# A perceiver block on one core: the way up's first rooms, its opening transposes, and who computes its weights' low parts

## The chip, the cores and the metric

The kernel runs on one core of one Trainium2 chip. Its time is the device time of one execution in microseconds (us), and the median of several executions is what counts. The core has a matmul engine (TensorE, PE in the profile, with PEld its weight loads), three engines for elementwise work (VectorE or DVE, ScalarE or ACT, GpSimd or POOL), a queue engine (SyncE or SP) that issues most transfers, and 16 DMA engines that move data between the large memory and the core's own memory. Each engine works through its own list of instructions in order and waits on semaphores for the others.

## The reference

The block takes `x` (32 sequences of 64 rows of 512 numbers, 2048 rows in all) and adds three things to it in turn.

```python
x = x + xattn(layernorm(x), ctx_2048, mask)        # cross attention
x = x + attn(layernorm(x), wq_a, ..., wo)          # latent attention, 16 heads
x = x + ffn(layernorm(x), gate_w, up_w, down_w, expert_weight, gamma, beta)

def ffn(h):
    logits = h @ gate_w                            # 8 experts
    scale = top_k(logits, 2).sum()
    hidden = square(relu(h @ up_w))                # 512 -> 2048: the way up
    shared = hidden @ down_w                       # 2048 -> 512: the way down
    y = shared + (h @ expert_weight) * scale       # the expert
    return (y - mean(y)) * rsqrt(var(y) + 1e-5) * gamma + beta
```

All of it is float32. The change lies in the last line's `ffn`.

## The kernel before, in words

**Precision.** A float32 number is kept as a high and a low part in a format that PE multiplies quickly. `split` makes them: ACT copies the number into the high part (rounding it), and another engine subtracts that from the number for the low part. A product of two such numbers takes three matmuls: high by high, low by high, high by low. `mm3` writes these three for the expert.

**Fewer products.** Large matrix products are computed in the manner of Strassen and Winograd, with seven products of blocks where eight would be needed. That costs sums ahead of them (`sums`, on POOL, or on `xc` for the way up in `sum_x`) and sums behind them (`combine`: one ACT copy and five DVE additions, lines 160 to 168, in four steps).

**Stages.** Cross attention and the latent attention's heads come first. Then come three products with a weight matrix each: the output projection (`wo`, tiles `op` and `oo`), the way up (`up`, tiles `up` and `uo`) and the way down (`down`, tiles `dp` and `do`). Each matrix lies in eight weight slots, each with seven blocks of high parts (`wh_...`) and seven of low parts (`wl_...`). `read_slot` brings a slot's seven blocks from the large memory into the room of its low parts, and `put_slot` then splits them in two pieces, of blocks 0 to 3 (1024 numbers in each of 128 rows) and 4 to 6 (768). The order in which a stage uses the slots is `ORDER = (0, 1, 5, 6, 7, 2, 3, 4)`. A slot is filled for the next stage while the stage before still runs on others.

**The way up.** It runs through four blocks of 512 rows (`b`), and in each through the eight slots (`n`, with slot `k = ORDER[n]`). One such unit (`up_seven`) is 42 matmuls of 256 columns, which are written to one of two sets of four accumulator banks. In unit 0 of a block, four of the seven sums first get five of their six products, so that the last part of `xr` is needed late. Behind each unit come `combine`, then relu and square on ACT (lines 1226 and 1227, tile `uo`), then for most slots the sums for the way down on POOL (`uw`), and the stores of `uo` and `uw`. `xr` are the high and low parts of the rows, made by `right(b, part)`: parts 0 and 1 are high and low of one half, 2 and 3 of the other; high parts are ACT's, low parts DVE's. Inside the first block, slots 3 to 7 in `ORDER` are split behind units 0 to 4. Inside the last block, the way down's first five slots are split behind units 2 to 6.

**The way down.** Its unit `u` is 21 matmuls, on a pair `hl` (high and low parts of a piece of `uo`, split by `left(u)`) and a slot of `down`. `left(0)`, `left(1)` and `left(2)` are written inside the way up's last block, behind units 3, 5 and 6; `left(u + 3)` is written at the way down's unit `u`.

**Settling.** `settle(n, ...)` writes `n` transposes into an accumulator bank that nobody reads. It stands ahead of the way up's first unit with eight of them, and ahead of units 5 and 32 of the way down with four.

**Order.** The kernel is written in a framework that orders the instructions of each engine by their place in the source and by a model of when they can start; so an instruction that is ready early may move ahead of others. `with after(ins)` or a `pins` argument holds an instruction behind another one of the same engine: the first pin is for ACT's copy, the second for the subtraction. The framework sets all semaphores. It also gives every tile its room: a pool's tags take their places in the order in which they are first used, and the rooms of a pool that is closed go to later pools. A write into such a room waits until the last reader of the tile before, a transfer among them, is done.

**The rooms of the way up.** The projection's pool `o_act` holds, in this order, `beb`, `mo`, `xt`, `o`, `p1`, `xn` (also `oT`), `xh`, `xl`. The tile `mo` is the expert's output and is written out from ACT's queue (line 1023); it is taken for the first time ahead of all others (`mos`, line 1070). When `o_act` is closed, the pool `f_act` takes the first of its rooms: three for `uo` of 5 KB a row and two for `up1`. The first `uo` then lies over `beb` and the start of `mo`; the later `u_x` rooms lie over `xh`, `xl` and what follows.

**The seam.** The last rows of the projection are turned (`o_t`, tiles `ops`, `oh`, `ol`, `oT`), the expert runs on them (`o_expert`, tiles `cpe`, `gs`, `mo`), and the way up begins with unit 0 of block 0. Its `right(0, 3)` waits for the expert's last product, since it writes over the expert's weights.

## Time and profile before

| what | us |
|---|---|
| median of three executions | 1104.6 |
| the three executions | 1100.06, 1104.6, 1104.91 |
| the profiled execution, its own time | 1098.9 |
| its span in the profile | 1096.7 |
| expert's last product begins | 772.9 |
| way up, first product to last | 773.1 to 931.0 |
| way up, last block: units begin at | 891.6, then every 4.95 |
| way down, first unit begins | 931.2 |
| granted PE clock, mean | 0.998 |

The three costliest groups that belong to the seam's stages, from the page's list (line, engine, operation, output and inputs, shapes, count, then busy time and the mean of one in ns):

```profile
L1156 PE MATMUL up<-xr,wh_up 128*128 128x256 f32 x896 | 157.6, 280 | 0.6 <-DVE uo L168 0.6
L1156 PE MATMUL up<-xr,wl_up 128*128 128x256 f32 x448 | 123.7, 280 | 0.0
L725 PE MATMUL dp<-wh_down,hl 128*128 128x256 f32 x448 | 124.5, 278 | 0.0
```

Matmuls overlap one another in the pipeline, so a mean of 280 ns is not the distance of one from the next. Behind the last bar of such a line stands the time for which the engine stood idle just before these instructions, and who ended it. In a timeline, a line has the start, the duration, the engine, the line of the source, the operation, the tiles, and in brackets the idle time before it. In a table of windows the columns are the window, its length, then the busy time and number of instructions of each engine, the granted clock, the DMA engines' share and GB/s.

### The profile page before, as it was taken

The page shows a single profiled execution, that of the slowest core. Times are in us where ns is not written, and L with a number is a line of the kernel's source. Part 1 is how long each engine was busy: PE and PEld are TensorE (multiplying, and loading weights), DVE is VectorE, ACT ScalarE, POOL GpSimd, SP SyncE. Part 2 cuts the span into 40 slices and gives each one's busy share as a digit, 9 for nine tenths or more (in the row PEclk, how much of TensorE's full clock was granted, in tenths as well). Part 3 has the DMA queues.
Part 4 walks back from the last instruction along what each step waited for, and adds up shares of the span by engine and source line. Part 5 has one row for each costly group of instructions (what it writes and reads, how often), then busy time and mean ns, then how long its engine had stood idle before and what let it go on. Part 6 is the DMA issues. An engine that isn't in the chain of part 4 may idle for free.

```text
span 1096.7 us, 26072 instructions
## 1 busy us (share of the span) xinstructions
PE 1066.9 (97%) x10201; PEld 983.6 (90%) x10201; DVE 769.0 (70%) x1369; ACT 546.1 (50%) x1051; POOL 508.1 (46%) x691
## 2 busy tenths in 40 slices
PE   8999999999999999999998999999999999999996
PEld 6667777679999999999988999999999999999996
DVE  5666666657666666656787866667785658898786
ACT  4444444533433444434475544445676567755553
POOL 2333333326788778874570000003238970065671
PEclk9999999999999999999999999999999999999999
DMA  8867666343776778655487776779646689998672
GB/s 259 263 216 231 206 212 203 124 161 121 260 234 245 260 247 294 249 207 195 160 324 276 263 241 213 231 235 359 218 156 202 221 247 366 310 309 257 206 232 79
DMA packets 195386, 254.67 MB, mean 232 GB/s; under 512 B 18544, under 2 KB 140032, under 8 KB 195264
## 3 DMA queue, kind: packets, MB, share of 16 engines
q1 hardware_dynamic: 190704, 240.92, 67.0%
q10 hardware_dynamic: 3456, 8.39, 2.2%
q0 software_dynamic: 1104, 3.70, 0.9%
q8 instruction: 80, 1.31, 0.5%
q14 instruction: 42, 0.34, 0.1%
HBM read 146.67 MB, written 106.30 MB: 231 GB/s over the span
## 4 chain that ended last, share of the span: by engine, by line
PE 59%; DMA 10%; POOL 9%; DVE 8%; issue 7%; ACT 5%; SPq 1%; DVEq 0%; POOLq 0%; ACTq 0%
PE up L1156 9%; PE pss L773 5%; PE psq L179 4%; PE psq L180 4%; PE psq L181 4%; PE op L725 3%; PE op L726 3%; PE op L723 3%; PE psv L817 3%; DMA hd<-uo 2%; PE pse L179 2%; PE pse L181 2%; PE pse L180 2%; DMA x1d<-xt 2%; DMA vd<-vw 2%
## 5 line engine op out<-in xcount | busy, mean ns | idle before, releaser
L755 DVE SCALAR_TENSOR_TENSOR qe<-pse,bqp,cq 64x256 f32<-64x256 f32 x256 | 123.7, 483 | 76.5 <-PE pse L181 70.7
L1156 PE MATMUL up<-xr,wh_up 128*128 128x256 f32 x896 | 157.6, 280 | 0.6 <-DVE uo L168 0.6
L1156 PEld LDWEIGHTS up<-xr,wh_up 128*128 128x128 f32 x896 | 137.5, 189 | 1.0 <-issue 0.7
L725 PE MATMUL op<-wh_wo,hl 128*128 128x256 f32 x448 | 124.4, 279 | 3.7 <-DVE hl L149 3.7
L723 PE MATMUL op<-wh_wo,hl 128*128 128x256 f32 x448 | 124.0, 280 | 0.6 <-ACT hl L147 0.6
L725 PE MATMUL dp<-wh_down,hl 128*128 128x256 f32 x448 | 124.5, 278 | 0.0
L723 PE MATMUL dp<-wh_down,hl 128*128 128x256 f32 x448 | 124.4, 278 | 0.0
L726 PE MATMUL dp<-wl_down,hl 128*128 128x256 f32 x448 | 124.3, 277 | 0.0
L149 DVE TENSOR_TENSOR hl<-c,hl 128x896 fp32r<-128x896 f32 x84 | 94.3, 1126 | 42.3 <-ACT hl L147 42.0
L1156 PE MATMUL up<-xr,wl_up 128*128 128x256 f32 x448 | 123.7, 280 | 0.0
L726 PE MATMUL op<-wl_wo,hl 128*128 128x256 f32 x448 | 123.5, 277 | 0.0
L147 ACT CAST hl<-c 128x896 fp32r<-128x896 f32 x84 | 79.0, 942 | 77.7 <-PE op L726 38.0
L179 PE MATMUL psq<-qa_hi,qh 128*128 128x256 f32 x384 | 112.5, 293 | 0.0
L180 PE MATMUL psq<-qa_hi,ql 128*128 128x256 f32 x384 | 106.4, 277 | 0.0
L181 PE MATMUL psq<-qa_lo,qh 128*128 128x256 f32 x384 | 106.2, 276 | 0.0
L725 PEld LDWEIGHTS op<-wh_wo,hl 128*128 128x128 f32 x448 | 84.3, 188 | 4.8 <-DVE hl L149 4.7
L723 PEld LDWEIGHTS op<-wh_wo,hl 128*128 128x128 f32 x448 | 83.6, 188 | 1.5 <-ACT hl L147 0.8
L723 PEld LDWEIGHTS dp<-wh_down,hl 128*128 128x128 f32 x448 | 84.6, 189 | 0.0
L725 PEld LDWEIGHTS dp<-wh_down,hl 128*128 128x128 f32 x448 | 84.1, 188 | 0.4 <-DVE hl L149 0.4
L1156 PEld LDWEIGHTS up<-xr,wl_up 128*128 128x128 f32 x448 | 84.2, 188 | 0.0
L726 PEld LDWEIGHTS op<-wl_wo,hl 128*128 128x128 f32 x448 | 84.1, 188 | 0.0
L726 PEld LDWEIGHTS dp<-wl_down,hl 128*128 128x128 f32 x448 | 84.1, 188 | 0.0
(233 smaller groups left out, 3146.6 us busy)
## 6 DMA issues: line engine op xcount, KB each, us to landing
c<-vd SPq DMA_DIRECT2D x58, 448.0 KB, 4.2
cx<-in_ctx SPq DMA_DIRECT2D x32, 512.0 KB, 4.6
vd<-vw SPq DMA_DIRECT2D x29, 512.0 KB, 3.6
hd<-uo SPq DMA_DIRECT2D x107, 128.0 KB, 3.3
hd<-uw SPq DMA_DIRECT2D x21, 512.0 KB, 3.3
dcw<-hd SPq DMA_DIRECT2D x18, 448.0 KB, 5.6
vd<-v SPq DMA_DIRECT2D x30, 256.0 KB, 3.5
wd_wo<-pw_wo SPq DMA_DIRECT2D x8, 896.0 KB, 4.9
```

Of the source, the lines that this page charges most:

```text
L147: copy = nc.scalar.copy(hi, src)
L149: return copy, engine.tensor_tensor(lo, src, hi.bitcast(FP), ALU.subtract)
L179: nc.tensor.matmul(ps, ah, bh, start=(j == 0), stop=False)
L180: nc.tensor.matmul(ps, al, bh, start=False, stop=False)
L181: nc.tensor.matmul(ps, ah, bl, start=False, stop=(j == n - 1))
L723: first = nc.tensor.matmul(ps[s // 2][:, s % 2], h[:, a], wh[:, b], start=(k == 0 and s % 2 == 0), stop=False)
L725: nc.tensor.matmul(ps[s // 2][:, s % 2], l[:, a], wh[:, b], start=False, stop=False)
L726: ins = nc.tensor.matmul(ps[s // 2][:, s % 2], h[:, a], wl[:, b], start=False, stop=last)
L755: rope = nc.vector.scalar_tensor_tensor(qe[64 * a : 64 * a + 64, :], pe[r, :], bqp[r, p : p + 1], cq[r, a, :], ALU.add, ALU.mult,)
L773: nc.tensor.matmul(ps[64 * j : 64 * j + 64, pj, b, :], qs[2 * pj + j][a][:, sl], kT[:, a, kt], start=(a == 0), stop=(a == 1),)
L817: nc.tensor.matmul(o, kv[a, i, :], t[a, bp, :], start=True, stop=True)
L1156: nc.tensor.matmul(ps[s // 2][:, s % 2], w[:, i, kk], xr[b, 2 * kk + low][:, j], start=(first and m == 0), stop=(last and m == len(parts) ...
```

## The change

Five edits, all around the way up.

1. `mo` isn't taken ahead of the others any more; its tag takes the place behind `xl`, and the tags between move down by its 4 KB a row.
2. `mm3` returns its last matmul; `o_expert` collects them, and the way up's opening transposes, now four, are held behind the last of them.
3. Slot `ORDER[2]` is split behind `right(0, 3)` instead of ahead of the last expert, and slot `ORDER[3]` right after it instead of behind unit 0, with its low part on POOL.
4. Slots `ORDER[5]` and `ORDER[7]` have their low parts on POOL too; they, `ORDER[4]` and `ORDER[6]` are split behind units 1 to 4 as before.
5. In the last block, the way down's slot `ORDER[4]` is no longer split behind unit 6 but at the way down's unit 1, and `left(2)` at its unit 0, held behind the last unit's square.

```diff
@@ mm3 @@
-            nc.tensor.matmul(ps, ah, bl, start=False, stop=(j == n - 1))
+            ins = nc.tensor.matmul(ps, ah, bl, start=False, stop=(j == n - 1))
+        return ins
@@ put_slot @@
-            def put_slot(k, what, pins=(None, None)):
+            def put_slot(k, what, pins=(None, None), engine=nc.vector):
...
-                    split(h[:, a], l[:, a], c[:, a], pins=pins)
+                    split(h[:, a], l[:, a], c[:, a], engine, pins)
@@ o_expert @@
-        mo = mos.pop(blk, None) or ap.tile([P, 2, D], FP, tag="mo", name=f"mo{blk}")
+        mo = ap.tile([P, 2, D], FP, tag="mo", name=f"mo{blk}")
...
-                mm3(pe[:, 0 : c.stop - c.start], [
+                made.append(mm3(pe[:, 0 : c.stop - c.start], [
...
-                ])
+                ]))
@@ the projection @@
-    mos = {0: ap.tile([P, 2, D], FP, tag="mo", name="mo0")}
...
-    put_slot(ORDER[2], "up", pins=xT[2])
     for _ in o_expert(NB - 1, *xT):
         pass
+    ends = made[-1]
@@ up_seven @@
-                with after(settle(8, ps, wh[:, 0, 0], ident2, None) if b == 0 else None):
+                with after(settle(4, ps, wh[:, 0, 0], ident2, ends) if b == 0 else None):
@@ the way up @@
-        right(0, 3)
+        put_slot(ORDER[2], "up", pins=(xT[2][0], right(0, 3)))
+        put_slot(ORDER[3], "up", (xT[2][0], None), nc.gpsimd)
...
-                if b == 0 and n < 5:
-                    put_slot(ORDER[n + 3], "up", pins=pins)
-                if b == NB // 2 - 1 and 1 < n < 7:
+                if b == 0 and 0 < n < 5:
+                    put_slot(ORDER[n + 3], "up", *((pins,) if n % 2 else ((act, None), nc.gpsimd)))
+                if b == NB // 2 - 1 and 1 < n < 6:
                     put_slot(ORDER[n - 2], "down", pins=pins)
...
-                if b == NB // 2 - 1 and n == 6:
-                    left(2, pins=(done[0], done[-1]))
@@ the way down @@
+            if u == 0:
+                left(2, pins=pins)
...
-            if u in (4, 6, 8):
-                put_slot(ORDER[3 + u // 2], "down")
+            if u in (1, 4, 6, 8):
+                put_slot(ORDER[max(4, 3 + u // 2)], "down")
```

More of the change, by code (lines that the diff above doesn't have):

```diff
@@ L1024, in o_expert @@
         yield
-    xr, xc, xw = {}, {}, []
+    xr, xc, xw, made = {}, {}, [], []
     def read_x(b, kk, room=None, behind=None):
```

## The prediction

> **What bounds the kernel.** I began with the page: TensorE (PE) is busy nearly throughout, so nothing can be won but its idle stretches and its pace.

> ```profile
> span 1096.7 us, 26072 instructions
> PE 1066.9 (97%) x10201; PEld 983.6 (90%) x10201; DVE 769.0 (70%) x1369; ACT 546.1 (50%) x1051; POOL 508.1 (46%) x691
> ```

> Of the 29.8 us in which PE is idle, the view of waits puts only one in the stage that the change touches: `PE up L1156 <- DVE uo L168: 0.6`. So I looked at the pace: way up's products in windows of 10 us, and then PE's timeline inside two of them.

> ```profile
> 786.00:796.00 10.00, 10.00 (x87) 10.00 (x86) 1.00 0.46 129
> 826.00:836.00 10.00, 10.00 (x91) 10.00 (x90) 1.00 0.60 203
> 856.00:866.00 10.00, 10.00 (x87) 10.00 (x86) 1.00 0.97 320
> ```

> ```profile
> 790.00 0.40 PE L1156 MATMUL up<-xr,wh_up 128*128 128x256 f32 x2
> ...
> 791.06 0.40 PE L1156 MATMUL up<-xr,wh_up 128*128 128x256 f32 x2
> ...
> 819.73 0.39 PE L1156 MATMUL up<-xr,wh_up 128*128 128x256 f32 x2
> ...
> 821.09 0.39 PE L1156 MATMUL up<-xr,wh_up 128*128 128x256 f32 x2
> ```

> PE is fully busy at a granted clock of 1.00 in all of them, yet 9 products take 1.06 us (117.8 ns each) in the first and 12 take 1.36 us (113.3 ns) in the second. There are two paces. Way up runs at the slow one from 773 to 809, at the quick one to 847, and slow again until 943. PE's timeline shows what moves it:

> ```profile
> 767.01 0.60 PE L713 MATMUL up<-ident,wh_up 128*128 128x128 f32 x4
> 773.04 0.27 PE L713 MATMUL up<-ident,wh_up 128*128 128x128 f32 x1
> 808.87 0.48 PE L1156 MATMUL up<-xr,wh_up 128*128 128x256 f32 x2 [0.57 <-DVE uo L168]
> 943.53 0.60 PE L713 MATMUL dp<-ident,wh_down 128*128 128x128 f32 x4
> ```

> At 943.5 four transposes in a row turn the slow pace to the quick one. Ahead of way up stands only one of the eight (773.04); seven ran earlier, between the expert's products. The stop at 808.87 also left the quick pace; one at 847 left the slow one.

> Then VectorE (DVE) at way up's start, in its timeline:

> ```profile
> 773.34 0.95 DVE L1065 TENSOR_TENSOR xr<-xp,xr 128x768 fp32r<-128x768 f32 x1
> 774.21 1.22 DVE L1065 TENSOR_TENSOR xr<-xc,xr 128x1024 fp32r<-128x1024 f32 x1
> 780.10 0.69 DVE L162 TENSOR_TENSOR uo<-up,up 128x512 f32<-128x512 f32 x1 [4.67 <-ACT up L160]
> ```

> The wait is put down to a copy that ended at 776.9. The last `mod<-mo` store is issued at 774.17 and takes 5.8 us: 780.0. `uo` and `mo` lie over one another in memory, so DVE waits for that store, and the delay runs through units 0 to 7 to the stop at 808.87.

> **Rooms, and the transposes.** With `mo` elsewhere, DVE can begin unit 0's sums when its products allow, at about 777.3; the new neighbour (`oT`'s stores, issued at 768.6 and 769.0, 5.6 us at most) is written out by 774.6, before unit 0's first copy at 776.5. The `mo` store now lies under a later `xr`, not written before 805. Gain for DVE: 2.8 us of waiting. PE gets only its stop: unit 7 took 813.39 - 807.78 = 5.61 us where its neighbours took 4.95, so 0.7 us.

> Transposes: four after the expert's last product, spaced 0.11 us, where one stood: 3 x 0.11 = +0.3 us. The seven that go had filled gaps (PE waited there for `oh` and `ol` anyway), so they give nothing back. If way up then starts at the quick pace, its first eight units take 8 x 42 x 0.1133 = 38.1 us, where the trace has 813.39 - 773.07 = 40.3. The stop is inside that 40.3, so pace and stop together give -2.2, and with the transposes **-1.9**. Bounds: 39.6 + 0.3 us, that is -0.4, if the slow pace stays; -1.9 if not. I take -1.9, because the four at 943.5 are the same instruction in the same number.

> [...]

> **Three low parts on GpSimd (POOL).** Each is one subtraction of 1024 and one of 768 elements. DVE does them in 1.22 + 0.95 = 2.2 us; three leave it. POOL has no such form here. Its nearest rows are 256 elements at 0.74 and 512 at 1.27, so 0.53 per further 256: 2.3 + 1.8 = 4.1 us a slot. That is alone. Against a working DVE, 256 elements cost it 1.25:

> ```profile
> 749.30 2.50 POOL L155 TENSOR_TENSOR xc<-xp 128x256 f32<-128x256 f32 x2 [10.44 <-DMA xp<-xTd]
> 775.21 1.52 POOL L155 TENSOR_TENSOR xc<-xp 128x256 f32<-128x256 f32 x2 [11.11 <-DMA x2d<-oo]
> ```

> Seven such are 8.8 us, the upper bound. I take 5.5, nearer to alone, since DVE is to have gaps. Against the need, with units of 4.76 us from 773.4: slot 3 (weights landed at 762.4, high part from 770.3 on ScalarE (ACT)) is low by 777, needed at 787.7; slot 5 has its high part after unit 2's squares, at about 790.4, and is low by 791.3 + 5.5 = 796.8, needed at 797.2; slot 7 is low by 806.3, needed at 807.3. All hidden, with 0.4 us to spare at slot 5; at 8.8 us slot 5 is 2.9 late and slot 7's second piece about 1. Behind them on POOL wait the sums `xc`, which waited for a landing until 775.2 and now run at 777 to 783 (needed after 800), and unit 5's `uw`, which in the trace began only at 808. POOL is idle from 781.7 to 808: that is the cover.

> Moving slot 2's low part behind `right(0,3)` on DVE: done at 777.5 instead of 773.4, needed at 782.9: nothing. But `right(0,3)` (ends 775.4, first needed there) now meets POOL. DVE's 1.22 became 1.75 beside POOL at 812.4, its 0.95 became 1.13: up to 0.7 us late. The first piece is needed first, so I take 0 and keep 0.7.

> [...]

> **Fewer splits at the end.** In the trace unit 2 of the way down starts at 936.1 and finds its `hl` long ready:

> ```profile
> 928.50 0.95 ACT L147 CAST hl<-hl 128x896 fp32r<-128x896 f32 x1
> ...
> 932.80 1.14 ACT L1227 ACTIVATE uo<-uo 128x512 f32<-128x512 f32 x2
> 933.84 1.77 ACT L147 CAST wh_down<-wl_down 128x1024 fp32r<-128x1024 f32 x2
> ```

> Now this split is pinned behind the last unit's squares. DVE, free of one `hl` part (1.0), does that unit's sums at 932.0 to 934.35. ACT squares from 934.0 to 936.2, then the high part to 937.1, the low part on DVE to 938.15. Unit 2's second product needs it at 936.2: **+2.0 us** of standing, where before nothing stood. Bounds: 0 if the squares come 2 us earlier; 3.0 if another 0.95 us split is put ahead. Behind it on ACT the splits for units 3 and 4 end at 938.8 and the moved weights' high part (1.77) at 940.6, the low part (2.1) by 942.7; unit 4 then starts at about 943: no further wait. The reads keep their places in the queues.

> **Sum**: -1.9 + 0 + 2.0 = **+0.1 us**, about no change. On the profiled execution (1098.9 us around its span of 1096.7) that is 1099. But this one was the fastest: 1098.9, 1100.06, 1104.6 and 1104.91 have a mean of 1102.1, under the median of 1104.6. I put the forecast there: **1102 us**, its own range 1098 to 1106.

> Forecast, 0.50: as summed.

> Rival 1, 0.22, faster: the quick pace holds. Units 16 to 31 take 79.1 us in the trace; at 38.6 a block of eight (the second block's time, its small stop at 847 included) they take 77.3, and without stops 76.2: -1.8 to -3.0. The way down's first five units give 12.27 - 11.9 = -0.4. If the split at its end also costs nothing, the whole is -4.1 to -5.3, 1097 to 1098. Against it: the stop at 847 came out of the second block's own order (DVE stood 3.8 us for POOL's `uw`), which the change leaves as it is.

> Rival 2, 0.14, slower: GpSimd's parts come late. Deciding point: slot 5 low after 797.2, that is over 5.9 us a slot. At 8.8: 2.9 + 1 + 0.7 for `right(0,3)`, with 3.0 at the way down: -1.9 + 7.6 = +5.7, 1108. For it: 2.50 for two beside a busy DVE; against: the 26 us gap of POOL, and DVE's relief.

> Rival 3, 0.14: the transposes don't set the pace. Then -0.4 + 2.0 = +1.6, 1104.

> **Range** 1096 to 1109: from rival 1 with a lucky pace to rival 2. About 0.5% (5.5 us) is what a measurement of this kernel can tell from no change; from 1104.6 that is 1099.1 and 1110.1. Below: most of rival 1 and a tail of the forecast, 0.27. Above: the upper part of rival 2 against the median and other stops, 0.15. Between: 0.58.

> **What would show it.** PE's timeline with four transposes between the expert's last and way up's first product, then 91 products in 10 us; DVE's first sums near 777.5; POOL's subtractions near 2.5 and 2 us; a wait of PE for `hl` some 5 us into the way down. I am wrong if the first eight units still take 40 us, if PE waits for a `wl_up` of POOL, or if no wait stands at the way down's unit 2.

## The result, and the profile after

The changed kernel takes 1111.55 us in the median, the kernel before 1103.55 beside it: a ratio of 1.0078, 95% interval 1.0061 to 1.0095. So it is slower by some 8 us, where I had forecast no change. The profiled execution took 1109.51 us, its span against that of before:

```profile
span 1107.7 us, 26068 instructions
```

I cut both spans at the same instructions of PE's timeline (the start of a unit is the start of its first product; "last turn" is the start of the last transpose of `ops`, after which only the expert's products come):

| stretch | before, us | after, us | difference |
|---|---|---|---|
| start to last turn | 765.64 | 764.38 | -1.3 |
| last turn to way up's first product (the seam) | 7.44 | 9.27 | +1.8 |
| way up, first block, units 0 to 6 | 34.71 | 33.79 | -0.9 |
| first block, unit 7 | 5.60 | 8.14 | +2.5 |
| second block | 38.63 | 39.65 | +1.0 |
| third block, fourth block | 79.15 | 79.51 | +0.4 |
| way down, units 0 to 4 | 12.72 | 20.31 | +7.6 |
| the rest | 152.8 | 152.7 | -0.1 |

The first row differs from execution to execution in every kernel (763.8 to 768.9 in those below) and has nothing to do with the change. The table adds up to 11.0 us, more than the 8 of the medians, since the profiled execution of before was among its fastest; so it shows where the time went, and not each row's share of the medians. Two thirds of the 11.0 lie in the last edit, at the start of the way down. The view of PE's waits names the two largest places:

```profile
PE dp L724 <- ACT hl L147: 4.7, 1, 4.7
PE up L1156 <- DVE uo L162: 2.4, 1, 2.4
```

The windows (length, PE's busy time and products, granted clock, DMA share, GB/s) show the rest:

```profile
766.00:768.00 2.00, 1.87 (x8) 0.55 1.03 386
768.00:770.00 2.00, 2.00 (x12) 0.59 1.04 405
770.00:772.00 2.00, 2.00 (x19) 1.00 1.07 403
786.00:796.00 10.00, 10.00 (x91) 1.00 0.38 105
826.00:836.00 10.00, 10.00 (x87) 1.00 0.84 279
...
940.00:945.00 5.00, 0.59 (x3) 0.87 0.84 243
945.00:950.00 5.00, 5.00 (x24) 0.50 1.13 312
```

The same two stretches of before, one in the seam and one in the way down:

```profile
768.00:770.00 2.00, 2.00 (x19) 1.00 1.06 398
945.00:950.00 5.00, 5.00 (x47) 1.00 1.07 353
```

The quick pace came as forecast (91 products in 10 us from 786) and was gone in the second block (87, where before had 91). And a thing that no step of mine held: the granted clock halves in the seam and again after the stop in the way down. There PE counts as busy, but does 12 and 24 products where the kernel before does 19 and 47.

PE's timeline has the four transposes in their place and the two stops:

```profile
773.29 0.60 PE L714 MATMUL up<-ident,wh_up 128*128 128x128 f32 x4
...
815.58 0.35 PE L1156 MATMUL up<-xr,wh_up 128*128 128x256 f32 x1 [2.41 <-DVE uo L162]
...
944.41 1.22 PE L724 MATMUL dp<-wh_down,hl 128*128 128x256 f32 x4 [4.66 <-ACT hl L147]
```

DVE's timeline answers for the first of them, POOL's beside it:

```profile
773.49 0.96 DVE L1066 TENSOR_TENSOR xr<-xp,xr 128x768 fp32r<-128x768 f32 x1 [1.05 <-PE cpe L181]
774.37 1.77 DVE L1066 TENSOR_TENSOR xr<-xc,xr 128x1024 fp32r<-128x1024 f32 x1
776.06 3.17 DVE L149 TENSOR_TENSOR wl_up<-wl_up,wh_up 128x1024 fp32r<-128x1024 f32 x2
779.15 0.68 DVE L162 TENSOR_TENSOR uo<-up,up 128x512 f32<-128x512 f32 x1
...
807.15 1.81 DVE L1066 TENSOR_TENSOR xr<-xp,xr 128x768 fp32r<-128x768 f32 x1 [2.02 <-ACT xr L1068]
808.88 2.87 DVE L1066 TENSOR_TENSOR xr<-xc,xr 128x1024 fp32r<-128x1024 f32 x1
811.68 1.49 DVE L1066 TENSOR_TENSOR xr<-xp,xr 128x768 fp32r<-128x768 f32 x1
813.10 1.74 DVE L1066 TENSOR_TENSOR xr<-xc,xr 128x1024 fp32r<-128x1024 f32 x1
814.76 1.27 DVE L162 TENSOR_TENSOR uo<-up,up 128x512 f32<-128x512 f32 x2
```

```profile
794.34 4.21 POOL L149 TENSOR_TENSOR wl_up<-wl_up,wh_up 128x1024 fp32r<-128x1024 f32 x2 [7.40 <-ACT wh_up L147]
805.73 4.94 POOL L149 TENSOR_TENSOR wl_up<-wl_up,wh_up 128x1024 fp32r<-128x1024 f32 x2 [7.18 <-ACT wh_up L147]
```

Four low parts of `xr` stand in a row on DVE, 7.6 us from the first's start to the sums, and only then come the sums of unit 6, whose products ended at 807.4. In the kernel before the order was two low parts, unit 6's sums (808.6), two low parts:

```profile
806.30 0.96 DVE L1065 TENSOR_TENSOR xr<-xp,xr 128x768 fp32r<-128x768 f32 x1
807.17 1.23 DVE L1065 TENSOR_TENSOR xr<-xc,xr 128x1024 fp32r<-128x1024 f32 x1
...
808.63 0.69 DVE L162 TENSOR_TENSOR uo<-up,up 128x512 f32<-128x512 f32 x1
...
811.39 1.13 DVE L1065 TENSOR_TENSOR xr<-xp,xr 128x768 fp32r<-128x768 f32 x1 [0.35 <-PE up L1156]
812.44 1.75 DVE L1065 TENSOR_TENSOR xr<-xc,xr 128x1024 fp32r<-128x1024 f32 x1
```

The second block's first product needs the accumulators of unit 6, so PE stands until 815.6.

ACT's timeline answers for the second stop:

```profile
931.30 1.79 ACT L147 CAST wh_down<-wl_down 128x1024 fp32r<-128x1024 f32 x2
...
936.62 1.06 ACT L147 CAST wh_down<-wl_down 128x1024 fp32r<-128x1024 f32 x1 [3.27 <-DMA wl_down<-wd_down]
937.59 1.15 ACT L1227 ACTIVATE uo<-uo 128x512 f32<-128x512 f32 x2
938.63 1.14 ACT L1228 ACTIVATE uo<-uo 128x512 f32<-128x512 f32 x2
...
941.34 1.15 ACT L1227 ACTIVATE uo<-uo 128x512 f32<-128x512 f32 x2
...
943.43 0.92 ACT L147 CAST hl<-hl 128x896 fp32r<-128x896 f32 x1
```

The split of `ORDER[4]`, which is no longer pinned, moved up to 931.3, and that of `ORDER[5]`, which had no pin before either and ran at 940.1 there, moved up behind it: its first piece stands at the head of ACT's list for 3.27 us until its weights land. Behind it wait the squares of unit 6 (937.6) and unit 7 (941.3), and only then comes `left(2)` (943.4), which unit 2 of the way down needs.

### The profile page after: what moved, and what is told of

Its sections match the earlier page's. It is cut to its first block, busy times and chain, and to the rows that moved or that the text cites. A ratio compares the mean times of both kernels' runs of the same rounds, so it can differ in the third digit from the quotient of the medians.

```text
span 1107.7 us, 26068 instructions
## 1 busy us (share of the span) xinstructions
PE 1071.5 (97%) x10197; PEld 987.3 (89%) x10197; DVE 765.8 (69%) x1363; ACT 545.6 (49%) x1051; POOL 519.9 (47%) x697
## 4 chain that ended last, share of the span: by engine, by line
PE 64%; DVE 8%; POOL 7%; DMA 7%; issue 7%; ACT 5%; SPq 0%; DVEq 0%; POOLq 0%; ACTq 0%
PE up L1156 9%; PE pss L774 5%; PE psq L179 4%; PE psq L180 4%; PE psq L181 4%; PE op L726 3%; PE op L727 3%; PE op L724 3%; PE dp L726 3%; PE psv L818 3%; PE dp L724 3%; PE dp L727 3%; PE pse L179 2%; PE pse L181 2%; PE pse L180 2%
## 5 line engine op out<-in xcount | busy, mean ns | idle before, releaser
L1156 PE MATMUL up<-xr,wh_up 128*128 128x256 f32 x896 | 157.3, 280 | 2.4 <-DVE uo L162 2.4
L1156 PEld LDWEIGHTS up<-xr,wh_up 128*128 128x128 f32 x896 | 137.3, 189 | 2.6 <-issue 2.6
L1156 PE MATMUL up<-xr,wl_up 128*128 128x256 f32 x448 | 124.2, 281 | 0.3
L147 ACT CAST hl<-c 128x896 fp32r<-128x896 f32 x84 | 78.9, 942 | 81.7 <-PE op L727 32.6
L1156 PEld LDWEIGHTS up<-xr,wl_up 128*128 128x128 f32 x448 | 84.2, 188 | 0.9 <-POOL wl_up L149 0.9
```

The source lines that it names most:

```text
L147: copy = nc.scalar.copy(hi, src)
L1156: nc.tensor.matmul(ps[s // 2][:, s % 2], w[:, i, kk], xr[b, 2 * kk + low][:, j], start=(first and m == 0), stop=(last and m == len(parts) ...
```

## The experiments

Medians and ratios are against the kernel before, run on the same chip (1102.1, 1101.8 and 1103.2 us in the three batches). In the expectations "the first six units" of the way down is the stretch from the first unit's start to the sixth's, which is units 0 to 4 of the table above; the seam of 18.4 or 20.2 us is counted from the last output unit's first product. A "slot 3", 5 or 7 is `ORDER[3]`, `ORDER[5]` or `ORDER[7]` of the way up, and "the fourth slot" is `ORDER[4]` of the way down.

### left(2) back in the last block

```diff
+                if b == NB // 2 - 1 and n == 6:
+                    left(2, pins=(done[0], done[-1]))
...
-            if u == 0:
-                left(2, pins=pins)
```

> The changed kernel with left(2) put back where it was before (behind unit 6's squares of the last block); the fourth slot's split stays behind unit 1 of the way down, without a pin. My theory: the first six units of the way down took 20.3 us in the changed kernel and 12.7 before, because left(2) runs behind the last unit's squares, and those stand on ACT behind two weight splits that the planner put ahead of them, one of which waits for a landing. With left(2) early, nobody waits for it: the six units fall to 12.7 to 13.5 us, the wait of PE for hl (4.7) is gone, the granted clock stays at 1.00 there, and the time falls by about 7 us to 1104. Rival A (the splits alone are to blame, wherever left(2) stands): the squares of units 6 and 7 are still late on ACT, unit 3 of the way down waits instead, six units of 16 us or more, 1108. Rival B (the clock falls here for another reason): no wait of PE, but a granted clock under 0.8 at 940 to 950.

1104.99 us, ratio 1.0016 [0.9995, 1.0036]. The way down's stretch is 12.80 us, PE waits for no `hl` there, and the clock is 1.00. By the ratios, 6.8 us of the 8.6 are back with this one move. Rivals A and B fall: a split (933.0) still runs ahead of unit 6's squares and one piece of another (938.3) ahead of unit 7's, and PE doesn't wait for `hl`. But ACT no longer stands for a landing there, so this run doesn't show what that wait would cost with `left(2)` early.

### The freed splits pinned

```diff
-                put_slot(ORDER[max(4, 3 + u // 2)], "down")
+                put_slot(ORDER[max(4, 3 + u // 2)], "down", pins=pins)
```

> The changed kernel, but the weight splits of the way down (slots 4 to 7) are pinned behind the last unit's squares, so that ACT does the squares of units 6 and 7 and left(2) ahead of them. This is the order that my prediction assumed. My theory: PE's wait for hl shrinks from 4.7 to the 2 to 2.5 us that I had predicted, the granted clock falls less or not at all, and the first six units take 15 to 16 us where the changed kernel took 20.3: 1107. Rival A (left(2)'s pin alone is to blame, the order of the splits doesn't matter): the wait stays at 4.5 or more and the six units at 20, 1111. Rival B (the clock falls at any stop there): wait of 2 to 2.5, but six units of 18 or more, with a granted clock of 0.5 to 0.6 in some window.

1106.3 us, ratio 1.0034 [1.0014, 1.0054]; the stretch is 15.11 us, the clock 1.00 throughout it, PE's waits 1.6 for `hl` and 0.4 for its low part. This is the order on ACT that my prediction had taken for granted, in ACT's timeline:

```profile
937.08 1.14 ACT L1228 ACTIVATE uo<-uo 128x512 f32<-128x512 f32 x2
938.12 0.93 ACT L147 CAST hl<-c 128x896 fp32r<-128x896 f32 x1
938.95 1.15 ACT L1227 ACTIVATE uo<-uo 128x512 f32<-128x512 f32 x2
...
941.04 0.92 ACT L147 CAST hl<-hl 128x896 fp32r<-128x896 f32 x1
```

The squares follow one another and `left(2)` comes at 941.0. Both rivals fall. The pin alone costs 15.1 - 12.7 = 2.4 us, where I had 2.0.

### The fourth slot's split back, left(2) not

```diff
-                if b == NB // 2 - 1 and 1 < n < 6:
+                if b == NB // 2 - 1 and 1 < n < 7:
...
-            if u in (1, 4, 6, 8):
-                put_slot(ORDER[max(4, 3 + u // 2)], "down")
+            if u in (4, 6, 8):
+                put_slot(ORDER[3 + u // 2], "down")
```

> The changed kernel with the fourth slot's split back where it was (behind unit 6 of way up's last block), while left(2) stays behind the last unit's squares. The planner then puts the later slots' splits behind the hl of units 2 to 5, where the kernel before had them. Theory: left(2)'s pin alone costs the 2.0 to 2.5 us that I had predicted (15 us for the first six units, as with the splits pinned), and the other 5 us came from the freed splits that ran ahead of the squares: 1106. Rival A: the pin alone costs it all, 20 us, 1111. Rival B: the pin costs nothing when ACT is in the old order, 12.7 us, 1104.

1108.11 us, ratio 1.0049 [1.003, 1.0068], and 17.58 us: between theory and rival A, so neither number holds. No split waits for a landing ahead of `left(2)` any more, but the fourth slot's still stands between the squares of unit 6 and unit 7 (937.9 to 939.6). PE waits 2.6 us for `hl`, and that stop is followed by a granted clock of 0.70 from 945 to 950. One split of 1.77 us ahead of the squares thus took the stretch from 15.1 to 17.6, clock included, and the second with its landing to 20.3. These steps are from one execution each: the four later kernels that have the last edit as it is take 19.3 to 21.8 us for this stretch, with 2.9 to 4.5 us of ACT waiting for the landing.

### The eight movable transposes back

```diff
-                with after(settle(4, ps, wh[:, 0, 0], ident2, ends) if b == 0 else None):
+                with after(settle(8, ps, wh[:, 0, 0], ident2, None) if b == 0 else None):
```

> The changed kernel with settle of eight transposes, free to move, as before: seven go into the gaps between the expert's products, one stands ahead of way up. Theory on the clock: without the seven, PE idles 2.3 us between 763.5 and 766.4 and the granted clock falls to 0.55 for 3.5 us, which costs 1.8 us; with them the granted clock stays at 1.00 from 764 to 772 and the stretch from the last output unit to way up's first falls from 20.2 to 18.4 us. Rival (the clock falls because of the pause itself or by chance, transposes or not): a granted clock under 0.7 in that stretch and 20 us. Theory on the pace: with one transpose ahead of way up instead of four, units 0 to 6 of its first block go at 4.95 us again (117.8 ns a product) where four gave 4.76. Rival on the pace (something else in the change made it quick, such as the wait of DVE for the store that is gone): units of 4.76. Both theories together: 1.8 gained, 1.0 to 1.3 lost, 1111; with the rival on the pace, 1109.7.

1112.2 us, ratio 1.0091 [1.0061, 1.0121]. The seam is 7.44 us from the last turn, as before, at a clock of 1.00 from 762 to 774. Units 0 to 6 go at 4.95. Both theories hold in their place. The way down's stretch, 20.3 in the changed kernel, is 21.8.

### The transposes alone, on the kernel before

```diff
-                with after(settle(8, ps, wh[:, 0, 0], ident2, None) if b == 0 else None):
+                with after(settle(4, ps, wh[:, 0, 0], ident2, ends) if b == 0 else None):
```

> The kernel before, with the transposes alone as in the change: four in a row after the expert's last product, none in the seam ahead of it. Theory on the pace: units 0 to 6 of way up's first block take 4.76 us each where the kernel before took 4.95, so 1.3 us less over the seven. Theory on the seam: without the seven, the stretch from the last output unit's last product to way up's first takes 7.7 us where the granted clock holds and 9.2 where it falls to about 0.55 (7.4 before); both were seen in kernels that lack them (7.7 in two, 9.2 in two), so the fall hits or misses by the moment. Net -1.0 or +0.5: 1101 to 1103. Rival (the wait of DVE for the store, which this kernel still has, set the pace, not the transposes): units of 4.95, and 0.3 to 1.8 lost, 1103 to 1104.

1102.12 us, ratio 0.9999 [0.9985, 1.0014]. Units 0 to 6 take 33.42 us (4.76 each but the first) against 34.71: the rival falls, since DVE's wait for the store is still there. The seam takes 7.75 at a clock of 1.00. What is won (1.3) is lost again: 0.3 in the seam, 0.5 at unit 7 (6.07, a stop of 0.9), and 0.9 in the second block, which runs at the slow pace after that stop.

### The rooms alone, on the kernel before

```diff
-        mo = mos.pop(blk, None) or ap.tile([P, 2, D], FP, tag="mo", name=f"mo{blk}")
+        mo = ap.tile([P, 2, D], FP, tag="mo", name=f"mo{blk}")
...
-    mos = {0: ap.tile([P, 2, D], FP, tag="mo", name="mo0")}
```

> The kernel before, with the rooms alone as in the change (mo apart from uo). Theory: DVE begins unit 0's sums near 777.5 to 779 and no longer at 780.1 after a wait of 4.7 for the store; PE had only one stop of 0.57 from it at unit 7, so 0.5 to 0.7 us is won at unit 7 (5.6 to 4.95) and nothing else; the pace of the first block stays 4.95. 1101.5 to 1102. Rival (the wait for the store held the slow pace): units of 4.76, 1100. Rival 2 (another neighbour takes its place): DVE or ACT waits for another store at 771 to 780, same time as before or more.

1099.63 us, ratio 0.9987 [0.9968, 1.0006]. Unit 7 takes 4.95 (5.60 before), and DVE's first sums come 4.8 us after way up's start (7.0 before) and wait for PE, for no store. The prediction's 0.7 us is there, the pace is 4.95 as expected; the time itself can't be told from no change.

### Both, with the seam's transposes kept

The same edit of the rooms, and the transposes as follows.

```diff
+                if b == 0:
+                    settle(8, ps, wh[:, 0, 0], ident2, None)
+                with after(settle(4, ps, wh[:, 0, 0], ident2, ends) if b == 0 else None):
-                with after(settle(8, ps, wh[:, 0, 0], ident2, None) if b == 0 else None):
```

> The kernel before with three things: the eight movable transposes as they were (seven go into the seam's gaps), four more in a row behind the expert's last product, and mo's room moved. The splits all stay on DVE and at their old places. Theory: the seam keeps its granted clock of 1.00 and takes 7.4 + 4 x 0.11 = 7.9 us, units 0 to 6 take 4.76, unit 7 takes 4.8 to 5.0, the way down's first six units 12.7: 1.3 + 0.7 - 0.4 = 1.6 us less than the kernel before, 1100.5; if the quick pace then holds in the blocks after, up to 3 less. Rival (pace is chance): units of 4.95, 1101.5 to 1102.5.

1099.62 us, ratio 0.9975 [0.9956, 0.9994]: the two parts of the change that win anything in a trace, and together a version that beats both kernels, if by little. What each adds can't be told from the medians: the rooms alone had 1099.63. Seam 7.87, units 0 to 6 33.42, unit 7 4.77, way down 12.56, as expected.

### Slot 7's low part on DVE again

```diff
-                    put_slot(ORDER[n + 3], "up", *((pins,) if n % 2 else ((act, None), nc.gpsimd)))
+                    put_slot(ORDER[n + 3], "up", *(((act, None), nc.gpsimd) if n == 2 else (pins,)))
```

> The changed kernel with the last of the three moved low parts (the slot put behind unit 4, for unit 7's sake) on DVE again, with the pins of the others; two stay on GpSimd. Theory: at 807 to 815 GpSimd's two subtractions and its uw sums run beside DVE's four low parts of xr, which take 1.5 to 2.9 us there and 0.95 and 1.22 alone; PE waits 2.4 us for DVE and unit 7 of the first block takes 8.1 us. With the low part on DVE, the parts of xr take 1 to 1.5 us each, unit 7 takes 4.8 to 5.6 us, and as the stop is gone the second block keeps the quick pace (38.6 us where the changed kernel took 39.7): together 3 to 4 us, 1108. Rival (DVE simply has too much to do there, wherever the subtraction runs): unit 7 takes 7 us or more again, the wait is for DVE, 1111.

1110.22 us, ratio 1.0072 [1.0046, 1.0098]. Unit 7 takes 6.94: 1.2 less, not the 2.5 to 3.3 that my theory asked for, and PE still waits 2.0 for the sums. The first two low parts of `xr` are down to 0.95 and 1.22, the second two take 1.06 and 1.75, but all four still stand ahead of the sums. The second block ran at the quick pace (38.17), as the theory had it, but behind a stop and not for want of one. The rival's number all but holds (6.94 for 7), and its reason has to be sharpened: not how much DVE has to do, but in which order, as the next run shows. A second, smaller thing shows in PE's timeline, at unit 5:

```profile
800.96 0.39 PE L1156 MATMUL up<-xr,wl_up 128*128 128x256 f32 x1 [0.46 <-POOL wl_up L149]
```

### The sums ahead of the second pair of low parts

```diff
+        stores, was = [], []
...
-                    late = right(b + 1, 3)
+                    late = right(b + 1, 3, (None, was[-1]) if b == 0 else (None, None))
...
                 pins = (act, done[-1])
+                was.append(done[-1])
```

> The changed kernel, but the second pair of xr's low parts in way up's first block is pinned behind the sums of the unit before, which is the order that DVE had in the kernel before; the three low parts stay on GpSimd. In the changed kernel the planner had put all four low parts of xr (7.9 us beside GpSimd) ahead of the sums of the unit at 802.7, and PE stood 2.4 us for their room; with one low part back on DVE the order was the same and the unit still took 6.9 us. Theory (the order on DVE is what stops PE): PE's wait of 2.4 is gone or under 0.7, unit 7 takes 5 to 6 us where it took 8.1, 2 to 3 us less, 1109. Rival (GpSimd slows DVE there whatever the order): the two low parts ahead of the sums still take 4.7 us and the sums that follow are late; unit 7 takes 7 us or more, 1111.

1108.38 us, ratio 1.0062 [1.0041, 1.0082]. Unit 7 takes 5.97, and the wait of 2.4 is down to pieces of 0.2 to 0.5. DVE's timeline:

```profile
807.01 2.87 DVE L1066 TENSOR_TENSOR xr<-xc,xr 128x1024 fp32r<-128x1024 f32 x1
810.26 0.69 DVE L162 TENSOR_TENSOR uo<-up,up 128x512 f32<-128x512 f32 x1 [0.38 <-ACT up L160]
...
812.58 1.04 DVE L1066 TENSOR_TENSOR xr<-xp,xr 128x768 fp32r<-128x768 f32 x1
```

The low part ahead of the sums is as slow as before (2.87), with POOL's subtraction beside it; still 2.2 of the 2.5 us are back. So the order is the larger cause here, POOL's work beside DVE the smaller.

### Slots 5 and 7 on DVE, slot 3 on GpSimd

```diff
-                    put_slot(ORDER[n + 3], "up", *((pins,) if n % 2 else ((act, None), nc.gpsimd)))
+                    put_slot(ORDER[n + 3], "up", pins=pins)
```

> The changed kernel with two of the three low parts (slots 5 and 7) on DVE again; only slot 3's stays on GpSimd. Theory: unit 5 of the first block (5.1 to 5.5 us in all kernels that have slot 5 on GpSimd, with a wait of PE for it) falls to 4.76, as slot 5's part now takes 2.1 us on DVE instead of 4.2 to 4.9 on GpSimd; unit 7 stays near 7 us, since the planned order (four low parts of xr ahead of the sums) is as in the changed kernel. Together 0.4 + 1.2 us less than the changed kernel, 1110. Rival (the extra 0.4 to 0.7 us of unit 5 is DVE's or ACT's lateness, not GpSimd's): unit 5 stays above 5.1.

1110.59 us, ratio 1.0064 [1.0039, 1.0089]. Unit 5 takes 4.76 where the kernels with slot 5 on GpSimd at the quick pace have 5.12 to 5.51: that loss is GpSimd's. Unit 7 takes 6.98, with the same four low parts in a row. So the order doesn't come from slots 5 and 7 on POOL. The kernels with transposes and rooms alone don't have it; what is left is the third edit, slot 2 later and slot 3 earlier. Which of those two it is wasn't tried.

### The changed kernel mended

`left(2)` as in the first experiment, the sums pinned as in the last experiment but one, and both sets of transposes.

> The changed kernel with its three losses mended as the earlier runs say: left(2) back behind unit 6, the second pair of xr's low parts pinned behind the sums, and the eight movable transposes put back beside the four pinned ones. The three low parts stay on GpSimd. Theory: seam 7.9 us at a clock of 1.00, units 0 to 6 at 4.76 but one of 5.1 to 5.5 (PE waits 0.2 to 0.5 for GpSimd's low part of slot 5), unit 7 at 6.0, way down's first six units 12.7: 1101 to 1102, about 1.5 to 2 us above the kernel before with transposes and rooms alone (1099.6), since the move to GpSimd and the later slot 2 bring nothing. Rival (the low parts on GpSimd and the freed DVE are worth something once the losses are gone): 1099 or less.

1102.18 us, ratio 0.9994 [0.998, 1.0009]. The theory's time, but not by its sum: the seam is 7.87 and the way down 12.35, but units 0 to 6 go at 4.95 although five transposes run right ahead of them. So the transposes are no certain means (below). The rival falls, although the lost pace took 1.3 us from this kernel: a gain from the low parts on GpSimd doesn't show in the median.

### Four transposes ahead of the third block too

On top of the kernel with both, a `settle(4, ...)` pinned behind the second block's last product (`prev` collects way up's products).

```diff
-                with after(settle(4, ps, wh[:, 0, 0], ident2, ends) if b == 0 else None):
+                with after(settle(4, ps, wh[:, 0, 0], ident2, ends if b == 0 else prev[-1]) if b in (0, 2) else None):
```

> The kernel before with mo's room moved, eight movable transposes, four more pinned ahead of way up's first block, and four more pinned ahead of its third block, which ran at the slow pace in all kernels built from the one before (39.57 us; the stop at the end of the second block turned it). Theory (four transposes in a row turn the slow pace to the quick one): third block 38.1 + 0.45 and fourth 38.1 where they took 39.6 each, 2.3 to 2.6 us less than the same kernel without them, 1097 to 1098 where that had 1099.6. Rival (the pace is set anew by some later stop, or by chance): both blocks at 39.6 and 0.45 lost, 1100.

1100.38 us, ratio 0.9981 [0.9964, 0.9998]. Way up's window in the third block, first without and then with these four:

```profile
856.00:866.00 10.00, 10.00 (x87) 1.00 0.99 320
```

```profile
856.00:866.00 10.00, 10.00 (x91) 1.00 0.98 318
```

The third block takes 38.18 us in place of 39.57, as the theory had it, and the fourth goes at 4.76 a unit too. But the fourth with the step into the way down takes 39.50 for 39.57: PE gets there sooner and then waits 1.3 us for DVE's additions (`up`, L163), where it had no such wait. The kernels with `left(2)` back, with pinned splits and with the fourth slot back also ran their third block quick or nearly so (38.1 to 38.8 us), and waited 1.6 us at the same place. The 1.4 us of the third block alone are too little for the ratios, which show no gain (0.9981 and 0.9975).

## Why the prediction was wrong, by its own steps

**"Fewer splits at the end: +2.0", with 3.0 as the bound. This is the step that failed most.** The term itself was right: with the order it assumed, the runs give 2.4. What failed is the sentence that put the splits "behind it on ACT", with "no further wait". `ORDER[4]`'s split lost its place behind unit 6 and got no pin, and the next one had none, so the planner was free to run both early, and the second could only wait for its weights there (3.27 us). A bound of one more split of 0.95 us was no bound for that. The change paid 7.6: 2.4 for the pin, about 2.5 for one split ahead of the squares, and 2.7 for the other with its landing (differences of single traces, see the spread above). Cut the other way, in the profile itself, 4.7 of the 7.6 are the stop (unit 1 takes 7.20 for 2.47) and 2.9 the halved clock after it (unit 2 takes 4.92, unit 3 2.98).

**"-2.2 for pace and stop together."** The pace was right: 4.76 a unit behind four transposes, and the transposes alone show it (-1.3 over units 0 to 6). That the stop at unit 7 would be gone was right for the rooms (5.60 to 4.95) and wrong for the change: I carried DVE's order of before into the new kernel, and the planner made another one. Unit 7 went from 5.6 to 8.1; with the old order pinned it takes 6.0. The second block then lost its quick pace (+1.0).

**"Hidden, with 0.4 us to spare at slot 5."** A slot took 4.2 us alone and 4.9 beside DVE, less than the 5.5 I took. But slot 5's part began at 794.3 and not at 791.3, since its high part was late on ACT, and was low at 798.55; the need was 797.2. That was my own deciding point for the slower rival, met for a reason that I hadn't named: its start, not its length. It cost 0.4 (unit 5 took 5.12). Slot 7's part, low at 810.7 and not at 806.3, was later still, and the weight loads of unit 7 waited 0.2 and 0.35 us for it.

**"The seven that go ... give nothing back."** In five of the eight kernels without them the seam is 7.73 to 7.76, 0.3 above the 7.44 of before, just as summed. In the changed kernel and two more it is 9.2 to 9.3, at a halved clock. In the six kernels that have them, the one before among them, it is 7.4 to 7.9 and the clock is 1.00. So they were worth up to 1.5 us as cover for the clock (the last section has the windows).

**"DVE's first sums near 777.5."** They came at 779.15: the low parts of `xr` and of slot 2 ran beside POOL's sums and took 5.9 us for the 4.3 that they take alone. As expected, PE didn't wait for it.

The time of before had been read well (1102 in my sum, medians of 1101.8 to 1103.6 in the later batches), so the error lies in the sum of +0.1 and not in what it was added to. Of the rivals, the one that held the transposes for idle fell (units of 4.76), the faster one lost its pace at unit 7's stop, and the slower one had the right side and one of its places, but neither the largest place nor its price. (The faster rival's 12.27 us for five units of the way down is 12.37 in the trace, which changes nothing.)

## What to carry to other kernels

Where a framework orders the instructions, taking away a pin or moving a call is a change of order on that engine, and its price is that of the worst order the planner may choose: write the new order out, engine by engine, before adding up durations, and pin what must not move ahead, above all work that waits for a landing. Work that fills a pause of PE may be what keeps its clock up (1.00 in the seam of all six kernels that have these transposes there, halved in three of the eight without them); before it is removed, add the pauses around it and put the cost of a halved clock for some 3.4 us (1.5 us here) into the range. A gain made ahead of a handover counts only if the engine on the other side is ready sooner too.

## What the runs showed of the hardware

**The clock after a pause.** Two kernels with the same pauses of PE in the seam (1.28, 1.03 and 0.50 us between starts), the one with `left(2)` back and the one with pinned splits; PE alone, columns as above:

```profile
768.00:770.00 2.00, 1.78 (x13) 1.00 0.80 313
770.00:772.00 2.00, 2.00 (x19) 1.00 0.82 306
```

```profile
768.00:770.00 2.00, 1.78 (x9) 0.66 1.05 394
770.00:772.00 2.00, 2.00 (x12) 0.50 0.94 353
```

PE is as busy in both, yet the second does 9 and 12 products where the first does 13 and 19. In the changed kernel products stood 0.22 us apart from 766.1 to 769.5, 3.4 us long. The traces hold the moments at which the granted clock changes. In the changed kernel's it is 0.50 three times ahead of the last products, from 585.30 to 588.72, from 766.21 to 769.62 and from 943.70 to 950.53: once, once and twice 3.413 us long, and the three falls are 53 and 52 such steps apart. The two kernels above cut into such steps, counted from the clock changes of each one's own trace, first the one that kept its clock, then the one that lost it:

```profile
762.49:765.90 3.41, 2.52 (x22) 1.00 1.01 423
765.90:769.31 3.41, 2.32 (x16) 1.00 0.97 376
```

```profile
761.83:765.24 3.41, 3.06 (x26) 1.00 1.01 425
765.24:768.65 3.41, 1.78 (x11) 1.00 1.01 407
```

The same pauses fall into two windows in the first (PE busy for 74% and 68%) and into one in the second (52%), and the clock falls at that window's end. In the changed kernel PE had been busy for 42%, 49% and 0% of the 3.41 us ahead of these three falls (1.42, 1.67 and 0.00 us). Busy time alone doesn't tell such windows from others: in the kernel before, cut into such steps back from its only fall (at 1091.44), the window from 586.27 has some 50% (1.72 us), and no fall follows it. With the eight movable transposes, the poorest window of the seam had 58% in the kernel before (1.98 us from 763.76); without them, in the changed kernel, it had the 49%. The stop at 939.75 in the changed kernel holds a whole window without a product, and the clock stayed halved for two windows behind it (943.70 to 950.53), the first of which began with the rest of the stop.

No run here moved the steps on purpose, so that their place decides is read from these traces and wasn't tested by itself; nor do they show how much busy time in a window is enough for a clock of 1.00.

**GpSimd beside DVE.** From 807.15 in the changed kernel, by what each takes alone (4.21; 0.95 and 1.22), an estimated 2.8 us of POOL's subtraction were left and 2.2 us of DVE's two; both were through at 811.75, 4.6 us later, the last 1.1 of them beside POOL's next sums. That is nearer to 5.0, one after the other, than to 2.8, side by side. Elsewhere it was otherwise: in the kernel before, from 811.39 on, DVE's two took 2.8 us beside POOL for the same 2.2, while POOL was busy for 2.5 of them.
